# Window values of six sequences: one wide projection per half, kept in DRAM, in place of four narrow ones in each sequence's own turn

## The chip, the cores and the metric

The kernel runs on one core of a Trainium2 chip. The metric is the device time of one execution in microseconds (us); the figure that is compared is the median of several executions. The core has five engines that each run their own list of instructions strictly in order and meet only at semaphores: PE (TensorE, matrix products into PSUM), DVE (VectorE), ACT (ScalarE), POOL (GpSimd) and SP (SyncE, which here only issues DMAs). [...]All data is float32, and each float32 matrix product shows as two PE records in the profile.

## The reference, cut to what matters

One decoder layer on x of shape (8, 256, 256), that is eight sequences of 256 rows and 256 channels: self-attention, cross-attention to a context of the same shape, and a mixture of eight experts, each followed by a sum with its input and a layer norm.

```python
# self-attention: three attentions with the same queries q, weighted by a gate
a1 = _attn(q, k1, v1, causal=True)     # latent keys and values
a2 = _attn(q, ks, vs, causal=False)    # 64 selected rows
a3 = _attn(q, kw, vw, causal=True)     # "window" keys and values
kw = (x @ w_wink)...                   # rope on 64 of 96
vw = (x @ w_winv).reshape(B, T, 16, 32)   # 256 -> 512 channels: 16 heads of 32
out = (g[:, 0] * a1 + g[:, 1] * a2 + g[:, 2] * a3) @ w_proj
x = _layernorm(x + out)
x = _layernorm(x + cross_attention(x, ctx))       # 16 heads of 16
# experts: all eight are computed for every row
h = relu(einsum('btd,edh->bteh', x, W1) + b1)     # 256 -> 1024
y = einsum('bteh,ehd->bted', h, W2) + b2          # 1024 -> 256
x = _layernorm(x + sum over e of router[e] * y[e])
```

The change concerns only `vw = x @ w_winv`. It depends on the layer's input and on one weight, and on nothing that is computed before it.

## The kernel before, in words

**Threads and a planner.** The kernel is written as some thirty generators ("threads"), each a sequence of instructions for one part of the work. When the program is built, a planner (class `Machine`, L119 to L255) walks through them with a small model of each engine's time. At each step it finds for every engine the instruction that could start earliest; among those within 0.1 us of it, it takes the one with the lowest rank number. The result is one fixed list per engine. The hardware then runs these lists in order, so an instruction that is late on the chip holds up all that stands behind it on its engine. A thread may also yield a number, which becomes its rank, or a condition (`seen(...)`) that holds it until another thread has set a mark.

**The ranks.** The self-attention and cross-attention threads of sequence s run at about 1 to 7 plus 4 times s (`AHEAD = 4`, L36), so a lower sequence goes first. `context()` (L1154) has rank 60: it projects keys and values of the context for all eight sequences and keeps them in DRAM. `finish()` has 50. `experts()` (L1387) has 99, so its products fill whatever time PE has left.

**What a sequence needs.** `project()` (L843) handles a sequence in four groups of four heads. For a group it makes q, the window keys and the selected keys, marks `heads`, and then makes the window values of the group: it claims one of two buffers `vw` (128 x 2 x 128), multiplies the two halves of the rows (i) by the group's 128 columns of `wvw` in four products with 128 columns each (k is the half of the contraction), into a PSUM bank `pv`, and copies that to `vw` on DVE or ACT, whichever is free first (`copied`, L294). `products()` (L1063) later multiplies the softmax weights `pa` with `vw` (L1105), with the selected values `vs` and with the latent values `vl`, and then releases `vw`. For the first sequence (s = 0) the weights are turned on PE (`pt`); for all others they are written to DRAM and read back turned, by SP's DMAs `pr<-pr` and `pa<-pr` (`by_dram`, L581; `turned`, L623).

**Buffers that the change touches.** The pool tag "side" has one buffer of 128 x 512; `context()` uses it for `kc` and `vc`, `second()` (L1215) for the cross-attention's queries `qc`, and `fetch()` (L1193) for `vc`. The tag "turn" has two buffers of 128 x 1024, and every rotary step uses one (`turn`, L548): DVE writes it, POOL reads it. The selected values of a sequence or a pair of them leave through a buffer `sv` of its own (L717).

**DMAs.** Every DMA is issued by SP, in one list, and an issue that waits for a buffer holds up the ones behind it. The expert weights come as 256 loads of 512 KB, with two buffers for the halves of W1 and two for those of W2.

Of the kernel before, what the change touches and what calls it, by code (L numbers as in the profile page):

```python
# [17 lines left out]
P = 128  # L18
# [14 lines left out]
NEG = -1e30  # L33
LOWEST = -3.4028234663852886e38
QSCALE = 1.0 / math.sqrt(DH)
AHEAD = 4  # L36
ENGINES = {
    mybir.EngineType.PE,
# [220 lines left out]
def decoder_layer(ctx: ExitStack, tc: tile.TileContext, a: dict, out: bass.AP):  # L259
# [13 lines left out]
    def mm(out, lhsT, rhs, start=True, stop=True, share=1):  # L273
        us = 2 * 0.00084 * max(free_size(rhs), free_size(lhsT)) / share
        return Op(
            "PE",
            us,
            [out],
            [lhsT, rhs],
            lambda: nc.tensor.matmul(out, lhsT, rhs, start=start, stop=stop, skip_group_check=share > 1),  # L280
            lag=0.17,
        )
# [5 lines left out]
    def group(ops, extra=0.0):  # L288
        op = Op("PE", sum(o.us for o in ops) + extra, [], [], lambda: [o.issue() for o in ops], lag=0.17)
        op.writes = list(dict.fromkeys(k for o in ops for k in o.writes))  # L290
        op.reads = list(dict.fromkeys(k for o in ops for k in o.reads))
        return op
# [15 lines left out]
    def mtile(shape, name):  # L308
        return mtile_(shape, "m", name)
# [30 lines left out]
    def kp(x):  # L340
        return x.rearrange("(k p) c -> p k c", p=P)
# [312 lines left out]
    def selection(s, d):  # L654


        xr = xrs[s]
        yield seen("raw", s)
        sc = one([1, T], "sc", "sc")
        yield m.claim(sc)  # L660
        pi = mtile([1, T], "pi")
        yield group([tr(pi[:, bass.ts(i, P)], d["gi"][:, i, 3:4]) for i in range(2)])
        yield copied(sc, pi)
        m.release(pi)
        left = one([1, T], "left", "left")
        for i in range(KEEP // 8):
            m8 = tiny("m8", [1, 8])
            src = left if i else sc
            yield V.max(m8, src)
            yield V.match_replace(left, m8, src, LOWEST)  # L670
        yield V.tensor_tensor(left, left, sc, ALU.not_equal)
        yield V.tensor_tensor_scan(sc, left, left, 0.0, ALU.add, ALU.max)
        yield V.tensor_tensor(sc, sc, left, ALU.mult)
        yield V.tensor_scalar(sc, sc, -1.0, None, ALU.add)
        m.release(left)
        pp = mtile([P, 2], "ppos")
        yield group([tr(pp[:, i : i + 1], sc[:, bass.ts(i, P)]) for i in range(2)])
        m.release(sc)
        pos = tiny("pos", [P, 2])
        yield V.tensor_copy(pos, pp)  # L680
        m.release(pp)
        hot = one([P, 2, KEEP], "left", "hot")
        for i in range(2):
            yield G.tensor_scalar(hot[:, i, :], iota, pos[:, i : i + 1], None, ALU.is_equal)

        n = s - lead(s)
        if n == 0:
            both = d["selT"] = one([P, 2, 2, KEEP], "selT", "selT")
            yield m.claim(both)
            d["users"] = 2  # L690
        else:
            yield lambda: "selT" in pro[s - 1]
            both = pro[s - 1]["selT"]
        pg = mtile([P, 2, KEEP], "psel")
        yield group(
            [
                mm(pg[:, k, :], xr[:, i, bass.ts(k, P)], hot[:, i, :], i == 0, i == 1)
                for k in range(2)
                for i in range(2)
            ]  # L700
        )
        m.release(hot)
        yield V.tensor_copy(both[:, :, n], pg)
        m.release(pg)
        done.add(("selected", s))
        if lead(s + 1) == s:
            return
        rows = (n + 1) * KEEP
        pv = mtile([P, H * VH], "pvs")
        yield group(  # L710
            [
                mm(pv[0:rows], both[:, k, 0 : n + 1].rearrange("p n s -> p (n s)"), wvs[:, k, :], k == 0, k == 1)
                for k in range(2)
            ]
        )
        used(lead(s))
        sv = one([P, H * VH], "sv", "sv")  # L717
        yield copied(sv[0:rows], pv[0:rows])
        m.release(pv)
        pro[lead(s)]["sv"] = dv = kept_in_dram([P, H * VH], f"sv{lead(s)}")  # L720
        yield dma(dv[0:rows], sv[0:rows])
        m.release(sv)
        done.add(("selected values kept", lead(s)))
# [119 lines left out]
    def project():  # L843
        for s in range(B):
            yield 2 + AHEAD * s
            d = pro.setdefault(s, {})
            for g in range(NHG):
                yield seen("latent", s)
                yield seen("parts", g)
                yield seen("latent weights")  # L850
                xT = xTs[s]
                h = {}
                for name, shape in (("q", [P, 3, T]), ("kx", [P, 3, KX]), ("vw", [P, 2, P])):
                    h[name] = two(shape, name, name)
                yield m.claim(h["q"], h["kx"])
                lT = d["lT"]

                pq = mtile([P, 2, T], "pq")
                yield group([mm(pq[:, i], wq[0:QL, 0, g, i], lT[0:QL, :]) for i in range(2)])
                yield from turn([h["q"][:, 0], h["q"][:, 1]], pq, T)  # L860
                m.release(pq)

                pk = mtile([P, 2, T], "pk")
                for i in range(2):
                    yield group([mm(pk[:, i], wkw[:, k, g, i], xT[:, k, :], k == 0, k == 1) for k in range(2)])
                yield from turn([window(h["kx"], 0), window(h["kx"], 1)], pk, T)
                m.release(pk)

                pq = mtile([P, T], "pqn")
                yield mm(pq, wq[0:QL, 0, g, 2], lT[0:QL, :])  # L870
                yield copied(h["q"][:, 2], pq)
                m.release(pq)

                pk = mtile([P, T], "pkm")
                yield group([mm(pk, wkw[:, k, g, 2], xT[:, k, :], k == 0, k == 1) for k in range(2)])
                yield copied(window(h["kx"], 2), pk.rearrange("p (c t) -> p c t", c=2))
                m.release(pk)

                ks = None
                if lead(s) == s:  # L880
                    two_ = lead(s + 1) == s
                    yield seen("selected", s)
                    if two_:
                        yield seen("selected", s + 1)
                        stash = kept[g] = four([P, 3, KEEP], "stash", "stash")
                        yield m.claim(stash)
                    ks = mtile([P, 3, 1 + two_, KEEP], "pks")
                    sel = d["selT"][:, :, 0 : 1 + two_].rearrange("p k n s -> p k (n s)")
                    yield group(
                        [  # L890
                            mm(ks[:, i].rearrange("p n s -> p (n s)"), wks[:, k, g, i], sel[:, k], k == 0, k == 1)
                            for i in range(3)
                            for k in range(2)
                        ]
                    )
                    if g == NHG - 1:
                        used(s)
                    if two_:
                        yield copied(stash, ks[:, :, 1])
                    own = ks[:, :, 0]  # L900
                else:
                    own = kept[g]
                yield from turn([h["kx"][:, i, P:N0] for i in range(2)], own[:, 0:2], KEEP)
                yield copied(h["kx"][:, 2, P:N0], own[:, 2])
                m.release(kept.pop(g) if ks is None else ks)
                heads[s, g] = h
                done.add(("heads", s, g))

                yield m.claim(h["vw"])
                pv = mtile([P, 2, P], "pv")  # L910
                yield group(
                    [
                        mm(pv[:, i], xT[:, k, bass.ts(i, P)], wvw[:, k, bass.ts(g, P)], k == 0, k == 1)
                        for i in range(2)
                        for k in range(2)
                    ]
                )
                yield copied(h["vw"], pv)
                m.release(pv)
                if g == NHG - 1:  # L920
                    m.release(d["lT"])
                done.add(("values", s, g))

    def latent_pairs(name):

# [543 lines left out]
    each(7, gates)  # L1469
    m.thread(5, selected_values())  # L1470
    m.thread(5, context())
    m.thread(5, fetch())
    m.thread(99, experts())
    m.thread(50, finish())
# [96 lines left out]
```

## Time and profile before

| | |
|---|---|
| median of 3 runs | 1673.97 us (1671.38 to 1674.11) |
| profiled execution | 1674.96 us, of which the span from first to last instruction is 1673.2 us |
| PE busy | 1609.5 us, 96% of the span |
| DVE, ACT, POOL busy | 1158.9, 583.8, 599.7 us |
| DMA | 330 MB, 57.6% of 16 engines |
| first expert product `ph` starts | 250.09 us |
| last product `ox` of the eighth sequence's cross-attention | 1512.1 us |

The page divides the span into 40 slices of 41.8 us and gives for each the busy tenths of each engine and the granted PE clock. A PE that is busy is not necessarily at its peak rate: while the clock is halved, the same products take longer and count as busy. "Idle before" and the views of waits give the time in which an engine had nothing running, and what released it. The kernel has three stretches: up to 250 us there are no expert products, since the first sequence has to pass both attentions first; from there to about 1510 us attention of the later sequences is mixed with experts; after that there are hardly any products but the experts'.

### The profile page before, as it was taken

The numbers are of one execution on the slowest core, as the hardware profiler recorded it, in microseconds if no ns is written. First come the engines' busy times: TensorE is split into PE (matmuls) and PEld (weight loads), VectorE is DVE, ScalarE is ACT, GpSimd is POOL, SyncE is SP. The second block draws the span as 40 slices with busy tenths as digits, with TensorE's granted clock in tenths as the row PEclk, the third lists the DMA queues.
The fourth block names the chain that finished last, engine by engine and source line by source line (L and its number), as shares of the span: only waits on it lengthen the run. The fifth ranks groups of instructions, "written<-read, shape, count | busy, mean of one in ns | idle before, by whom it ended". The sixth has DMA issues, their size and how long they took to land.

```text
span 1673.2 us, 31920 instructions
## 1 busy us (share of the span) xinstructions
PE 1609.5 (96%) x12040; PEld 1320.2 (79%) x12040; DVE 1158.9 (69%) x2577; ACT 583.8 (35%) x2114; POOL 599.7 (36%) x795
## 2 busy tenths in 40 slices
PE   6899789999999999999999999999999999999998
PEld 4778568887887778888888688878888778888887
DVE  4968678678789874887678884688767774544333
ACT  2464543244435430434434341244435341220000
POOL 3665753253534430334235332243335332120000
PEclk8999899999999999999999999999999999999999
DMA  6311416378648675655746676566656777585552
GB/s 218 117 50 47 166 69 217 120 245 284 233 141 291 245 248 192 211 205 189 252 172 234 241 249 227 151 238 211 226 196 221 248 257 251 154 307 153 161 156 96
DMA packets 185657, 329.96 MB, mean 197 GB/s; under 512 B 13200, under 2 KB 105504, under 8 KB 178336
## 3 DMA queue, kind: packets, MB, share of 16 engines
q1 hardware_dynamic: 185504, 327.92, 57.6%
q8 instruction: 96, 1.57, 0.4%
q14 instruction: 57, 0.47, 0.1%
HBM read 237.70 MB, written 90.19 MB: 196 GB/s over the span
## 4 chain that ended last, share of the span: by engine, by line
PE 83%; issue 7%; DVE 4%; DMA 3%; POOL 1%; SPq 1%; ACT 0%; POOLq 0%; DVEq 0%; ACTq 0%
PE ph L280 23%; PE py L280 22%; PE s L280 9%; PE o L280 4%; PE pk L280 3%; PE pyo L280 3%; PE ox L280 2%; PE pv L280 2%; PE sx L280 2%; DMA xpt<-prx 1%; PE pkm L280 1%; PE pks L280 1%; PE pq L280 1%; PE pt L286 1%; PE pkr L280 1%
## 5 line engine op out<-in xcount | busy, mean ns | idle before, releaser
L280 PE MATMUL ph<-xT,w 128*128 128x256 f32 x2048 | 475.2, 382 | 3.8 <-DVE pl L98 2.6
L280 PE MATMUL py<-w,h 128*128 128x256 f32 x2048 | 471.5, 381 | 0.0
L280 PEld LDWEIGHTS ph<-xT,w 128*128 128x128 f32 x2048 | 383.8, 190 | 70.2 <-issue 16.7
L280 PEld LDWEIGHTS py<-w,h 128*128 128x128 f32 x2048 | 383.7, 190 | 59.7 <-issue 7.7
L98 ACT ACTIVATE h<-ph,b 128x256 f32<-128x256 f32 x227 | 107.5, 473 | 391.5 <-PE ph L280 340.0
L98 DVE TENSOR_SCALAR h<-ph,b 128x256 f32<-128x256 f32 x285 | 136.9, 482 | 112.5 <-PE ph L280 109.6
L98 DVE SCALAR_TENSOR_TENSOR xr<-py,rw,xr 128x256 f32<-128x256 f32 x128 | 61.2, 478 | 174.7 <-PE py L280 174.6
L98 POOL TENSOR_TENSOR prx<-prx,sumsx 128x512 f32<-128x512 f32 x128 | 130.6, 1051 | 118.8 <-DVE sumsx L98 73.2
L98 ACT ACTIVATE prx<-sx,nmx 128x256 f32<-128x256 f32 x256 | 117.0, 486 | 43.3 <-DVE nmx L98 41.9
L98 POOL TENSOR_TENSOR pr<-pr,wpr 128x256 f32<-128x256 f32 (+2 forms) x128 | 129.4, 1042 | 0.0
L98 POOL TENSOR_TENSOR rstd<-var,nhalf 128x2 f32<-128x2 f32 x24 | 17.4, 725 | 310.0 <-DVE var L98 309.9
L98 ACT ACTIVATE pl<-pl,nmpl 128x128 f32<-128x128 f32 (+1 forms) x256 | 113.1, 446 | 30.6 <-DVE nmpl L98 29.9
L98 POOL TENSOR_TENSOR kx<-turn 128x64 f32<-128x64 f32 (+1 forms) x128 | 65.3, 527 | 162.6 <-DVE turn L98 156.9
L98 ACT ACTIVATE pr<-pr,nmpr 128x128 f32<-128x128 f32 (+1 forms) x256 | 113.2, 447 | 0.0
L98 DVE TENSOR_TENSOR pr<-s,causal 128x256 f32<-128x256 f32 x128 | 74.6, 583 | 41.0 <-PE s L280 34.6
L280 PE MATMUL s<-kx,q 32*128 32x320 f32 (+1 forms) x1536 | 96.1, 390 | 0.3 <-POOL kx L98 0.3
L98 POOL TENSOR_TENSOR pl<-pl,wpl 128x512 f32<-128x512 f32 x64 | 93.1, 1475 | 2.7
L98 POOL TENSOR_TENSOR q<-turn 128x256 f32<-128x256 f32 x64 | 45.8, 735 | 134.1 <-DVE turn L98 130.8
L280 PEld LDWEIGHTS s<-kx,q 32*128 32x128 f32 x1536 | 71.2, 189 | 17.8 <-issue 7.1
L98 DVE TENSOR_REDUCE nmx<-sx 128x2 f32<-128x512 f32 x128 | 79.1, 678 | 8.5 <-PE sx L280 8.5
L98 DVE TENSOR_TENSOR pl<-s,causal 128x256 f32<-128x256 f32 x128 | 74.3, 581 | 12.6 <-PE s L280 8.6
L98 DVE TENSOR_REDUCE nmpr<-pr 128x4 f32<-128x256 f32 (+2 forms) x128 | 80.5, 673 | 0.0
(217 smaller groups left out, 2385.1 us busy)
## 6 DMA issues: line engine op xcount, KB each, us to landing
w<-in_W SPq DMA_DIRECT2D x256, 512.0 KB, 4.2
pr<-pr SPq DMA_DIRECT2D x28, 1024.0 KB, 4.1
pa<-pr SPq DMA_DIRECT2D x28, 1024.0 KB, 6.9
prx<-prx SPq DMA_DIRECT2D x28, 1024.0 KB, 5.2
xpt<-prx SPq DMA_DIRECT2D x28, 1024.0 KB, 6.5
pl<-pl SPq DMA_DIRECT2D x28, 768.0 KB, 4.9
pb<-pl SPq DMA_DIRECT2D x28, 768.0 KB, 7.2
xT<-in_xT SPq DMA_DIRECT2D x8, 256.0 KB
```

The lines of the kernel that those rows point to most:

```text
L98: return Op(self.name, us, outs, ins, lambda: getattr(self.engine, kind)(*args, **kw))
L280: lambda: nc.tensor.matmul(out, lhsT, rhs, start=start, stop=stop, skip_group_check=share > 1),
L286: return Op("PE", 0.11, [out], [in_], lambda: nc.tensor.transpose(out, in_, ident[:n, :n]), lag=0.17)
```

## The change

The window values of sequences 0 and 1 are made as before. For sequences 2 to 7 (`EARLY = 2`) a new thread `values()` with rank 61 makes them ahead of time. As soon as the weights of the context are there (mark "ctx weights"), it loads the sequence's transposed input once more into a new buffer `vT`, and for each half of the rows makes one PSUM bank of 128 x 512 with two products (all 16 heads at once), copies it on ACT into the one "side" buffer, and writes it to DRAM (256 KB). `project()` then issues, in place of the four products and the copy, one DMA that reads the group's 128 columns of both halves into `vw`. To make room for `vT`, `sv` moves from a buffer of its own to one of the two "turn" buffers.

```diff
+EARLY = 2
 ...
-        sv = one([P, H * VH], "sv", "sv")
+        sv = two([P, H * VH], "turn", "sv")
 ...
                 yield m.claim(h["vw"])
-                pv = mtile([P, 2, P], "pv")
-                yield group([mm(pv[:, i], xT[:, k, bass.ts(i, P)], wvw[:, k, bass.ts(g, P)], k == 0, k == 1)
-                             for i in range(2) for k in range(2)])
-                yield copied(h["vw"], pv)
-                m.release(pv)
+                if s < EARLY:
+                    (the same as before)
+                else:
+                    yield seen("values kept", s)
+                    yield dma(h["vw"], vws[s][:, :, bass.ts(g, P)])
 ...
+    vws = {}
+
+    def values():
+        for s in range(EARLY, B):
+            yield 61
+            yield seen("ctx weights")
+            xT = one([P, 2, T], "vT", "vT")
+            yield dma(xT, kp(a["xT"][:, bass.ts(s, T)]))
+            d = vws[s] = kept_in_dram([P, 2, H * VH], f"vw{s}")
+            for i in range(2):
+                pv = mtile([P, H * VH], "pv")
+                yield group([mm(pv, xT[:, k, bass.ts(i, P)], wvw[:, k], k == 0, k == 1) for k in range(2)])
+                vw = one([P, H * VH], "side", "vw")
+                yield A.copy(vw, pv)
+                m.release(pv)
+                yield dma(d[:, i], vw)
+                m.release(vw)
+            m.release(xT)
+            done.add(("values kept", s))
 ...
     m.thread(5, context())
+    m.thread(5, values())
     m.thread(5, fetch())
```

More of the change, by code (lines that the diff above doesn't have):

```diff
@@ L909, in project @@
                 yield m.claim(h["vw"])
-                pv = mtile([P, 2, P], "pv")
[L911 to L917, printed above, removed]
-                yield copied(h["vw"], pv)
-                m.release(pv)
+                if s < EARLY:
+                    pv = mtile([P, 2, P], "pv")
+                    yield group(
+                        [
+                            mm(pv[:, i], xT[:, k, bass.ts(i, P)], wvw[:, k, bass.ts(g, P)], k == 0, k == 1)
+                            for i in range(2)
+                            for k in range(2)
+                        ]
+                    )
+                    yield copied(h["vw"], pv)
+                    m.release(pv)
+                else:
+                    yield seen("values kept", s)
+                    yield dma(h["vw"], vws[s][:, :, bass.ts(g, P)])
                 if g == NHG - 1:
@@ L922, in project @@
                 done.add(("values", s, g))
+    vws = {}
[11 more added lines that the diff above has]
+                yield A.copy(vw, pv)
+                m.release(pv)
+                yield dma(d[:, i], vw)
+                m.release(vw)
+            m.release(xT)
+            done.add(("values kept", s))
     def latent_pairs(name):
```

## The prediction

> **What bounds the kernel now.** I began with the page, parts 1 and 2.
>
> ```profile
> PE 1609.5 (96%) x12040; PEld 1320.2 (79%) x12040; DVE 1158.9 (69%) x2577; ACT 583.8 (35%) x2114; POOL 599.7 (36%) x795
> ...
> PE   6899789999999999999999999999999999999998
> ...
> PEclk8999899999999999999999999999999999999999
> ```
>
> PE is busy for 96% of the span. Of its 63.7 us of idle time (1673.2 - 1609.5) most lies in the first seven slices, and only there is the clock below 9. So I cut that stretch up and set a later one beside it (columns: stretch, then busy us of PE, weight loads, DVE, ACT and POOL, granted clock, DMA share, GB/s).
>
> ```profile
> 50.00:100.00 50.00, 44.29 (x390) 36.21 (x389) 43.26 (x116) 29.95 (x109) 37.90 (x53) 0.93 0.29 89
> 100.00:150.00 50.00, 47.31 (x518) 38.53 (x520) 38.43 (x105) 26.29 (x88) 29.57 (x36) 0.97 0.14 50
> 150.00:200.00 50.00, 42.39 (x347) 32.76 (x340) 36.10 (x74) 27.24 (x102) 32.67 (x45) 0.90 0.41 145
> 200.00:250.00 50.00, 42.20 (x432) 32.33 (x431) 36.87 (x80) 25.70 (x98) 26.82 (x34) 0.92 0.16 60
> ...
> 600.00:800.00 200.00, 197.81 (x1380) 164.22 (x1380) 142.78 (x328) 64.42 (x237) 63.41 (x83) 1.00 0.62 209
> ```
>
> From 50 to 250 us PE is idle for 5.7 + 2.7 + 7.6 + 7.8 = 23.8 us, and the halved clock takes (0.07 + 0.03 + 0.10 + 0.08) x 50 = 14 us more. Those 38 us are what work without a deadline could fill. From 600 to 800 us only 2.2 of 200 us are idle: there every us of PE work taken away is a us won. The waits of PE up to 260 us and after it say who causes the idle time (us in total, times, longest).
>
> ```profile
> PE ptx L286 <- DVE xr L98: 5.2, 1, 5.2
> ...
> PE plt L286 <- DVE lat L98: 5.1, 2, 2.7
> PE o L280 <- DMA pa<-pr: 4.4, 1, 4.4
> PE pt L286 <- POOL pr L98: 3.7, 3, 1.7
> ...
> PE sx L280 <- ACT prx L98: 1.9, 1, 1.9
> ```
> ```profile
> PE ox L280 <- DMA xpt<-prx: 4.5, 4, 1.9
> PE ph L280 <- DVE pl L98: 2.6, 2, 1.6
> ```
>
> Early there are waits of the first sequence's chain. Later there is nearly nothing, and no product `ph` or `py` ever waits for a weight's DMA.
>
> **Part 1: PE work removed.** Six sequences x 4 groups = 24 groups `pv` of 4 products (8 records). Their cost is the distance to the next group's start (a record's duration overlaps the next).
>
> ```profile
> 424.40 1.16 PE L280 MATMUL pv<-wvw,xT 128*128 128x128 f32 x8
> 425.49 0.71 PE L280 MATMUL pvl<-wkv,lk 32*128 32x128 f32 x8
> ```
> ```profile
> 301.48 1.88 PE L280 MATMUL pvs<-wvs,selT 128*128 128x512 f32 x4
> 303.20 1.05 PE L280 MATMUL pv<-wvw,xT 128*128 128x128 f32 x8
> 304.18 2.06 PE L280 MATMUL s<-kx,q 32*128 32x192 f32 x36
> ```
>
> That is 1.09 and 0.98 us; with 1.0, 24.0 us. All 24 lay behind 250 us, where experts fill PE, so all of it counts.
>
> **Part 2: PE work added.** 12 groups of two products 128 x 512. The group `pvs` has exactly this shape: 303.20 - 301.48 = 1.72 us, so 20.6 us. In the planned order all 12 stand before the first `ph`. If nothing is recovered, the trade is 20.6 - 24.0 = -3.4 us.
>
> **Part 3: what the added work covers.** I read this from the planned order of PE, wait by wait.
> - `ptx` (5.2 us, at 243 us): before, only the cross-attention's projection stood ahead of it; now `pk`, `pqn`, `pkm` and a context projection too, 0.86 + 0.43 + 0.87 + 1.73 (distances of starts) = 3.9 us.
> - `plt` of the second sequence (2.7 of the 5.1 us, at 117 us): a values group stands ahead of it, 1.7 us.
> - `sx` (1.9 + 0.7 us, at 188 us): a values group, the second sequence's `psel` and context work now stand between the `sx` groups, 2.6 us.
> - `pt` (3.7 us, at 67 us): POOL's constant fill of `xq` (2.80 us) stood before the first `pr` weighing and now stands behind it, 2.8 us. Against that, 4.5 us of other PE work (`pqn`, `pkm`, `xpv`, `pks`) that stood ahead of `pt` is replaced by one values group; it isn't lost, but the cover is thinner, so I count only 1.5 us.
> - `ox` (1.4 + 0.8 us): score groups stand between now, 1.5 us.
> - `o` (4.4 us, at 194 us): its values group stands behind it, so nothing.
>
> The sum is 11.2 us of idle time. For the clock there is a row and a rule. The row: after the 4.4 us wait the clock was 0.52 from 190 to 200 us, and `pv` at 198.32 took 1.87 us to the next start instead of 1.0; over 50 to 250 us it cost 14 us for 24 us of waits. The rule: the Trainium skill, "TensorE: Matmul & The Clock Gate", section "What's actually happening", says that the clock halves after an idle window of some 3.4 us and comes back after as much work. By it only the two waits above 3.4 us should cost, some 1.7 us each, 3.4 us in all; the row, 0.58 us of clock per us waited, would return 6.5 us for 11.2. The waits that I shorten are mostly below 3.4 us, so I take 3 us, nearer the rule: -11 - 3 = -14 us.
>
> **Part 4: what the added work costs elsewhere.**
> - ACT: 12 copies 128 x 512 at 0.585 us (row `vc<-xpv`), 7.0 us before 250 us, where ACT is busy for 109 of 200 us. ACT and DVE lose 24 copies of 0.372 or 0.424 us later. Cover: ACT's free half. But each copy waits for the one "side" buffer, and the softmax exponentials stand behind it on ACT. The nearest row is the context's `kc`, written by 16 ACT instructions into the same buffer: before `kc` work ACT and POOL sat idle for 9.4 us with no releaser shown and for 2.1 us until a DMA out of "side" (`cq<-qc`) had landed, 11.5 / 16 = 0.7 us for each. Bounds for 12 copies: 0 to 9 us. I take 3 us, since PE had other groups to run in most of these places.
> - SP: 18 more issues before 250 us and 24 later, 0.45 us each, 19 us of an engine with room. The `vT` load waits for PE to read the last one and the writes wait for ACT; behind them stand context loads and the second sequence's `pr` and `pa`. 0 to 5 us; I take 1.
> - The 24 reads of `vw` (128 KB) replace the products. Each waits for the products two groups earlier to release its buffer. In the planned order of SP each stands 11 to 44 entries ahead of the `pa` read that the same products need, and `pa` itself waits for a later release. Reads of 128 KB (`vs<-sv`) land in 3.0 us. So `o` isn't held up. A rule against it: the Trainium skill, "Perfetto Trace Analysis", "DMA Optimizations", warns that small DMAs (under 2 KB) have significant overhead; these rows are 512 B, those of `vs` 2 KB. By the row it costs 3 us of latency, by the rule perhaps twice that (an estimate); with at least one `pa` landing (6.9 us) of lead both come out at nothing.
>
> ```profile
> vs<-sv SPq DMA_DIRECT2D x16, 128.0 KB, 3.0
> ck<-kc SPq DMA_DIRECT2D x8, 256.0 KB, 2.0
> ```
>
> - DMA volume: 12 x 256 + 6 x 256 + 24 x 128 KB = 7.9 MB on 330 MB, most of it where the DMA share is 0.14 to 0.41. Nothing.
> - `sv` in "turn": five times a rotary buffer is held for a copy (0.6 us) and a write (2.4 us). Twice before 250 us the other buffer alone serves DVE and POOL; up to 2 us, I take 0. Later experts cover it.
> - The whole plan shifts, since it is one greedy list. Idle time after 260 us is 15 us before; I allow 4 us either way and take 0.
>
> **The sum:** -3.4 - 14 + 3 + 1 = -13.4 us against the profiled 1674.96 us (span 1673.2 and 1.8 around it), 1661.6. The median shown is 1.0 us lower; I forecast 1661.
>
> **The rivals.**
> - *Nothing is recovered (1666 to 1675).* The added groups take their full 20.6 us in a stretch where PE is already busy for 88%, and the waits only move behind them, since they come from latency the planner doesn't know. For it: the longest wait, `pa<-pr`, keeps its place. Against it: for the other four, work now stands ahead. Time: -3.4 + up to 4 of stalls, 1672.
> - *All of it is recovered (1645 to 1653).* The 20.6 us run inside the 38 us of idle and slow time. Then -24.0 counts alone, 1650. Against it: a group of 1.72 us in a gap of 1 us pushes the rest.
> - *Slower (1677 to 1700).* ACT is held at the "side" buffer. Each of the 12 copies waits until the write before it has landed (2.0 us by the `ck` row), and with it the exponentials behind it, so the first sequence's chain is late and new waits of PE open where there are no experts to fill them. The gain without stalls is 17.4 us, so it decides from 17.4 / 12 = 1.5 us of PE wait per copy; at 2.5 us it is +12.6 us, 1687. For it: ACT and POOL already idle before `kc`, and `context()` needs the same buffer 16 times. Against it: ACT has half its time free, and PE has the second sequence's work.
>
> **How the numbers follow.** Chances: forecast (1653 to 1666) 0.43, nothing recovered 0.25, all recovered 0.12, slower 0.20. A measurement of this kernel tells about 0.2%, 3.3 us, from no change; faster means below 1670.6. "Nothing recovered" is split evenly by it: 0.12 faster, 0.13 the same. So faster 0.67, same 0.13, slower 0.20. For 8 in 10 the range leaves out the lower half of "all recovered" and the upper part of "slower": 1649 to 1682. The likeliest case's own range is 1653 to 1666.
>
> **What would show it.** Right: 8 instead of 32 `pv` groups of 128 columns and 12 of 512, all before the first `ph`; PE idle from 50 to the first `ph` at 14 us or less; the wait of `ptx` near 1 us; no product `o` waiting for a read of `vw`; the first `ph` some 10 to 15 us later than 250 us, with more of the second sequence done. Wrong: ACT idle for over 1.5 us before the new copies on a DMA, PE idle before 300 us above 40 us, or `ph` waiting for weights because a `vw` read blocks SP.

## The result, and the profile after

The changed kernel took **1686.43 us** (median of 6 executions, 1680.44 to 1691.28), the kernel before beside it 1673.46 us (6 executions, 1671.38 to 1674.95). The ratio is **1.0077**, 95% interval 1.0056 to 1.0099: the change makes the kernel 0.8% slower, where 1661 us had been forecast. The profiled execution took 1691.28 us with a span of 1689.4 us, against 1674.96 and 1673.2 before.

The page's first two parts of the changed kernel, the lines that answer to those shown of before:

```profile
PE 1618.7 (96%) x11896; PEld 1312.4 (78%) x11896; DVE 1178.0 (70%) x2582; ACT 577.6 (34%) x2097; POOL 600.3 (36%) x795
...
PE   5989978999999899999999999999999999999998
...
PEclk8999989999899899999999999999999999999999
```

PE has 144 records fewer, as the removal of 24 groups of 8 and the addition of 12 groups of 4 make it, and yet it is busy for 9 us longer. The row of the clock says why: it now falls below 9 in two slices far behind the first `ph`, the eleventh and the fourteenth. The mean granted clock went from 0.986 to 0.977. A slower clock makes the same products longer, and they count as busy.

The stretches (columns as in the prediction: stretch, busy us of PE, weight loads, DVE, ACT and POOL, granted clock, DMA share, GB/s):

```profile
50.00:100.00 50.00, 42.34 (x348) 31.91 (x348) 40.03 (x108) 25.77 (x94) 31.52 (x41) 0.86 0.30 87
100.00:150.00 50.00, 50.00 (x505) 38.27 (x503) 38.61 (x113) 31.08 (x105) 28.29 (x40) 1.00 0.16 52
150.00:200.00 50.00, 48.38 (x436) 36.34 (x436) 38.27 (x75) 23.73 (x79) 23.48 (x33) 1.00 0.45 139
200.00:250.00 50.00, 38.77 (x319) 27.97 (x318) 26.62 (x57) 25.86 (x99) 28.12 (x33) 0.86 0.41 139
```

From 100 to 200 us PE hardly idles any more: there the added groups did what they were forecast to do. But from 50 to 100 and from 200 to 250 us it idles for 7.7 and 11.2 us, more than before (5.7 and 7.8), at a lower clock. From 45 us to the first `ph` (250.1 us before, 276.2 us now) 23.8 us of idle time and 13.7 us of clock (half of the time at half clock, from the trace's clock record) were lost before, 26.0 and 14.0 us after. Where both fall together and are counted once, that is 33.8 us before and 37.0 us after (the 38 us of the prediction counted that part twice). The first `ph` is 26 us later, which is the added work (20.6 us), one more group of the second sequence, and these 3 us. Nothing was covered on balance.

The waits of PE in the changed kernel, over the whole span (us in total, times, longest):

```profile
PE xpk L281 <- DVE pl L99: 6.5, 1, 6.5
PE ppos L287 <- DVE sc L99: 4.5, 1, 4.5
PE s L281 <- ACT prx L99: 4.0, 1, 4.0
PE o L281 <- ACT pr L99: 3.3, 1, 3.3
...
PE ptx L287 <- DVE xr L99: 2.3, 2, 1.7
```

The old waits did shrink: `ptx` from 5.2 to 1.7 us at its longest, and the waits from 40 to 280 us for `lat` and for `pa<-pr` are gone. Four others stand in their place. Two are early (`ppos` at about 93 us, `xpk` at 220 us), two are far behind the first `ph`. PE's instructions behind these last two (start, us, what, idle before and its releaser), and then the stretches around them (same columns as above):

```profile
423.22 1.00 PE L281 MATMUL s<-lx,q 32*128 32x128 f32 x9 [4.01 <-ACT prx L99]
...
563.47 1.51 PE L281 MATMUL o<-pa,vw 128*32 128x256 f32 x16 [3.30 <-ACT pr L99]
```

```profile
420.00:430.00 10.00, 6.78 (x48) 5.37 (x49) 6.34 (x12) 3.75 (x16) 1.30 (x2) 0.61 0.97 336
430.00:440.00 10.00, 10.00 (x87) 7.36 (x86) 6.34 (x14) 3.76 (x13) 5.41 (x6) 0.88 0.38 125
...
560.00:570.00 10.00, 6.70 (x64) 4.58 (x61) 9.86 (x22) 4.48 (x19) 3.12 (x4) 0.61 0.27 93
570.00:580.00 10.00, 10.00 (x64) 7.63 (x63) 6.80 (x13) 1.61 (x4) 4.22 (x4) 0.88 0.76 259
```

Each of the two waits, 4.0 and 3.3 us, goes with another (0.39 + 0.12) x 10 = 5.1 us of clock, some 0.5 us of it still within the wait. From 400 to 600 us, where before lost 3.1 us of idle time at full clock, the changed kernel loses 10.8 us of idle time and 10 us of clock. Two more stretches of half clock of 3.4 us each, from 961.5 and from 1337.0 us, are too short to show in the page's digits; before has one such, from 941.4 us. From the first `ph` to 1400 us idle time and clock, counted once, lost 18.6 us before and 36.3 us after: 3.8 us more of idle time (17.1 and 20.9) and some 14 us more of clock. So the ledger of the profiled pair: the trade -3.4, the early stretch +3, the late one +18, some +17 where +16.3 was measured.

### The profile page after: what moved, and what is told of

It reads as the page before. It is cut to its first block, busy times and chain, and to the rows that moved or that the text cites. A ratio compares the mean times of both kernels' runs of the same rounds, so it can differ in the third digit from the quotient of the medians.

```text
span 1689.4 us, 31698 instructions
## 1 busy us (share of the span) xinstructions
PE 1618.7 (96%) x11896; PEld 1312.4 (78%) x11896; DVE 1178.0 (70%) x2582; ACT 577.6 (34%) x2097; POOL 600.3 (36%) x795
## 4 chain that ended last, share of the span: by engine, by line
PE 77%; DVE 8%; issue 7%; DMA 4%; POOL 2%; SPq 1%; ACT 0%; POOLq 0%; DVEq 0%; ACTq 0%
PE ph L281 21%; PE py L281 21%; PE s L281 8%; PE o L281 4%; PE pk L281 3%; PE pyo L281 2%; PE pq L281 2%; PE sx L281 2%; PE ox L281 2%; DMA prx<-prx 1%; PE pks L281 1%; PE pv L281 1%; PE pkm L281 1%; PE pt L287 1%; DVE pr L99 1%
## 5 line engine op out<-in xcount | busy, mean ns | idle before, releaser
L281 PE MATMUL ph<-xT,w 128*128 128x256 f32 x2048 | 480.2, 385 | 0.4 <-ACT prx L99 0.4
L99 DVE TENSOR_SCALAR h<-ph,b 128x256 f32<-128x256 f32 x314 | 151.0, 482 | 115.8 <-PE ph L281 113.0
L99 ACT ACTIVATE h<-ph,b 128x256 f32<-128x256 f32 x198 | 93.5, 473 | 331.7 <-PE ph L281 302.3
L281 PE MATMUL s<-kx,q 32*128 32x192 f32 (+1 forms) x1536 | 93.9, 383 | 0.3 <-POOL kx L99 0.2
L99 DVE TENSOR_TENSOR pl<-s,causal 128x256 f32<-128x256 f32 x128 | 74.5, 582 | 11.2 <-PE s L281 9.5
```

The costliest lines, as they stand in the source:

```text
L99: return Op(self.name, us, outs, ins, lambda: getattr(self.engine, kind)(*args, **kw))
```

## The experiments

Three theories, named so in the expectations. **A**: the trade of work is as forecast, and what is lost is lost to new waits, because the plan made another order on all engines. **B**: the loss comes from the early stretch itself, from the shared buffer "side", from SP, or from the disturbed chain of the first sequence. **C**: the reads from DRAM cost time.

### One half of the change at a time

Removal alone: the 24 groups are replaced by reads, there is no values thread, and `sv` keeps its buffer. The rows are read from the weight, so the values of six sequences are not the right ones.

```diff
+                    yield dma(h["vw"], kp(a["w_winv"])[:, :, bass.ts(g, P)])
-    m.thread(5, values())
```

> The products and copies of the window values of sequences 2 to 7 are left out: the group's columns are read from the weight w_winv instead (same pieces of 512 B, same 24 DMAs), and no values are computed ahead, so those sequences' window attention uses wrong values. This is the removal alone. Theory A (the trade holds, and what was lost is new waits that any reshuffled plan can have): 24 us less, 1649, give or take 8 for the plan. Theory B (the loss is in the early stretch, from the shared buffer and SP's queue): 24 us less, 1649, closely. Theory C (the reads themselves cost: SP is blocked, or the groups had been useful filling): about 10 us less or nothing, 1663 to 1673.

Measured: 1670.66 us (1665.91 to 1674.41, 11 executions), ratio 0.998 (0.9967 to 0.9992). Only 3 us of the 24 came, where A and B expected them all; the time is one that C named.

Addition alone: the changed kernel with its values thread, but all sequences still compute their values themselves and nothing reads the rows in DRAM.

```diff
-                if s < EARLY:
+                if s < B:
```

> The values of sequences 2 to 7 are computed ahead and written to DRAM as in the change, but nobody reads them: every group still makes its own. This is the addition alone, sv in a rotary buffer included. Theory A: the 20.6 us of products without cover, 1694, give or take 8. Theory B: 20.6 us and some 16 us of waits in front of the first expert product, 1710. Theory C: about 20 us, 1694, closely. If the early gaps had covered the products after all: below 1685.

Measured: 1706.59 us (1703.89 to 1713.91, 4 executions), ratio 1.0197 (1.0166 to 1.0228): 33 us for 20.6 us of work. That is nearest to B's 1710. Each half comes out 12 to 21 us worse than its instructions. As both make a new plan, these two runs can't say whether the halves or the plan are to blame.

### The order alone

The plan charges 2.5 us for the way of a transfer. With 2.4 or 2.6 the kernel before does the same work in another order. The plan also decides anew what DVE and what ACT takes: with 2.4, 318 of the 512 `h` are made on DVE, before 285. "Order" below includes that.

```diff
-            end = self.transfers + 2.5
+            end = self.transfers + 2.4
```

> The kernel before with one number of the planner changed (the latency it assumes for a DMA, 2.4 instead of 2.5 us), so that only the order of instructions shifts; the work is the same. Theory A: the time moves by up to 8 us either way, and the single long waits of PE are other ones. Theories B and C: within 3 us of before, 1670 to 1677.

> The kernel before, whose planner takes 2.6 us for a transfer's way instead of 2.5: same work, another order. Theory A: 1680 to 1695, as with 2.4 (1689.87). If the order of before is nothing special: within 5 us of 1673.7.

Measured: with 2.4, 1689.87 us (1683.7 to 1693.32), ratio 1.0081 (1.0053 to 1.011); with 2.6, 1688.61 us (two executions), ratio 1.0091 (1.0066 to 1.0116). The order alone costs 15 to 16 us in both; for 2.4, theory A had allowed 8. With 2.4 the first `ph` stands at 252.8 us, so at most 3 us of it are in the early stretch. Most of it is clock: the mean granted clock is 0.978, in before 0.986, and 0.008 x 1689 us are some 13 us. Two of the waits of PE in that run, over the whole span:

```profile
PE ox L280 <- DVE pl L98: 5.3, 1, 5.3
...
PE sx L280 <- DVE pl L98: 4.7, 1, 4.7
```

Neither is there in before. The first stands at 960 us: one long wait in the midst of the experts' time, as the changed kernel has them. The order of before is better than both of its neighbours, and an edit that makes a new plan can lose it.

The changed kernel with the same two constants:

> The changed kernel with the same number of the planner changed (2.4 instead of 2.5 us). Theory A: another time than the changed kernel's 1686 by some us, anywhere from 1665 to 1690. Theories B and C: within 3 us of 1686.

> The changed kernel with 2.6 us instead of 2.5. Its distance to the kernel before with 2.6 us is the change with another draw of the order on both sides. By the pairs so far (+13 at 2.5, +9.5 at 2.4) between 0 and +15 us. If the change is worth its sum of -13 us and only the order of before hides it, it is below its partner in some pair.

Measured: with 2.4, 1699.41 us (1696.52 to 1701.16), ratio 1.015 (1.0133 to 1.0167), 9.5 us above its partner. With 2.6 one execution took 1716.66 us, 28 us above its partner's median; a second, of 1756.44 us, ran at a mean granted clock of 0.928 instead of 0.973 and is not compared. Both times lie above what had been expected (up to 1690, and up to 15 us over the partner). The change loses in each of three draws of the order. Three draws, one of them a single execution, are few beside a spread of 15 us, but they speak against the luck of before being the whole of it.

### The removal in the order of before

The plan still sees the group and its copy at their old costs. When it comes to issue them, the group issues nothing, and the copy issues the read. Every engine's list is then that of before, less the 24 groups and copies, plus 24 reads on SP where the copies stood; in the trace PE, DVE, ACT and POOL run their instructions in the order of before, but for those left out. The values are those of the removal alone, not the right ones.

```diff
+                    same = group([...])
+                    same.issue = lambda: None
+                    yield same
+                    both = copied(h["vw"], pv)
+                    for op in both:
+                        op.issue = lambda v=h["vw"], g=g: nc.sync.dma_start(out=v, in_=...)
+                    yield both
```

> The removal alone, like the run with reads only (1670.66 us, 3 us below before), but every engine's order stays that of before: the 24 groups and their copies are left out where they stood, and the 24 reads stand on SP where the copies stood. The values read are not the right ones. Theory A (the order of before is a rare good one, and reordering ate the removal's 24 us): about 1650 us, 1647 to 1654, the whole 24 us. Theory C (the reads themselves cost, as waits of the products or on SP): no better than the run with reads only, 1665 to 1675, with waits of `o` on the DMA of vw in the chain of waits.

Measured: **1652.56 us** (1652.37 to 1654.39), ratio 0.9879 (0.9861 to 0.9898), that is 21.0 us below before, where the same removal with a new plan brought 3. The page of this run:

```profile
PE 1587.3 (96%) x11848; PEld 1299.2 (79%) x11848; DVE 1153.5 (70%) x2568; ACT 578.6 (35%) x2099; POOL 599.7 (36%) x795
```

PE is busy for 22.2 us less than before. Theory C falls, since the 24 reads are all in this kernel. The 18 us between the two removals are the new order's. (`sv` keeps its own buffer in both, so the move of `sv` is not needed for such a loss.)

### The values in the experts' time

```diff
-            yield seen("ctx weights")
+            yield seen("normed", 0)
```

> As the changed kernel, but the values wait for the first sequence's normed rows instead of the context weights, so the 12 groups run in the experts' time and not in the early stretch. Nothing is covered by early waits, so the trade is -3.4 us. Theory A: the order shifts here too, for some +15 us: 1680 to 1690. Theory B (the loss comes from the early stretch: the shared buffer, the first sequence's chain): 1668 to 1673, as nothing early is touched, and the first ph near 250 us.

Measured: 1684.92 us (1684.44 to 1689.19), ratio 1.0077 (1.0054 to 1.01), the ratio of the changed kernel itself. The first `ph` starts at 252.0 us, so the early stretch is as before, and the loss is there all the same. One of its waits of PE, over the whole span, stands at 940 us:

```profile
PE sx L281 <- DVE pl L99: 8.0, 1, 8.0
```

From 600 to 1400 us this run idles for 15.4 us (before 11.6), and its clock is 0.98 from 600 to 1000 us. Theory B does not explain this kernel.

### The shared buffer

The changed kernel in its own order, but the rows on their way to DRAM lie in buffers that the experts use only later; the planner still books "side" for them. One copy becomes two of half the width, and one write two.

```diff
-                vw = one([P, H * VH], "side", "vw")
+                vw, more = like_side("vw0"), sb.tile([P, T], F32, tag="h", name="vw1", bufs=8)
```

> The changed kernel in its own order on every engine, but the rows on their way to DRAM lie in buffers that the experts use only later (two copies of 128 x 256 and two writes per group), not in side; the planner still books side for them, so that the order stays. If the shared buffer is a cause (ACT idle for 8.3 us before `vc` at 208 us until `ck` had landed, then PE idle for 6.5 us before `xpk`), both waits shrink and the time falls by 5 to 10 us, to 1676 to 1682. If the order alone is it, within 3 us of the changed kernel's 1686.4, since the same instructions stand in the same queues.

Measured: 1689.73 us (1684.88 to 1693.72), ratio 1.0098 (1.0079 to 1.0116), no better than the changed kernel. One of the waits of ACT from 45 to 276 us in this run, then one of PE's in the same stretch:

```profile
ACT vc L99 <- DMA ck<-kc: 9.7, 1, 9.7
```
```profile
PE xpk L281 <- DMA cT<-in_ctxT: 9.9, 2, 9.3
```

The pair of waits (208 to 220 us in the changed kernel, 203 to 216 us here) is still there, though no row of the new thread is in that buffer. It is `context()`'s own chain: `vc` waits until `kc` has left "side", and the `cT` load stands behind the issue of `ck` on SP. What SP waits for there, and what POOL does in that time (start, us, what):

```profile
SPq L272 <- POOL kc L99: 10.9, 1, 10.9
```
```profile
199.18 4.03 POOL L99 TENSOR_TENSOR prx<-prx,sumsx 128x512 f32<-128x512 f32 x4
...
204.78 4.02 POOL L99 TENSOR_TENSOR pr<-pr,wpr 128x512 f32<-128x512 f32 x4
208.77 0.59 POOL L99 TENSOR_TENSOR kx<-turn 128x64 f32<-128x64 f32 x2
209.33 1.26 POOL L99 TENSOR_TENSOR kc<-kc,keep 128x512 f32<-128x512 f32 x1
```

The masking of `kc` on POOL stands in the plan behind two weighings of 4.0 us each. So this price is the order's, not the sharing's.

### The whole change in the order of before

Now the added part is set in without the plan's knowledge: its instructions take no time and no buffers in the plan, and each is issued as soon as the plan has come to the time at which it could run. The rows lie in the experts' buffers, as above; the removed part is handled as in the removal in the order of before. These values are the right ones.

```diff
+                pv = unseen(ps, "m", 8, [P, H * VH], "pv8")
+                yield free_of_cost(group([...]), 0.0)
+                vw = [unseen(sb, "h", 8, [P, T], "vwh") for k in range(2)]
+                for k in range(2):
+                    yield free_of_cost(A.copy(vw[k], pv[:, bass.ts(k, T)]), 0.0)
```

> The whole change, right values, but with every engine's order that of before: the 12 groups of values, their copies, loads and writes are set in where the plan of before has come to by the time they can run, and are nothing to the planner; the reads stand where the copies stood, as in the run with reads in the order of before (1652.56 us). The rows lie in buffers that the experts use only later (tag h, two copies of 128 x 256 and two writes per group instead of one), so nothing waits for the buffer side, and sv keeps its own. Theory A (the change is as forecast and lost by the new order): 1652.6 + 20.6 added less what early waits cover (11 to 14 us) = 1659 to 1663. Nothing recovered: 1652.6 + 20.6 = 1673. Theory B (the addition disturbs the first sequence's chain wherever it is put): above 1675.

> The addition alone in the order of before: as the run with the whole change in that order, but the 24 groups pv and their copies are computed as before and nothing reads the rows kept in DRAM. The addition alone with its own new order cost 33 us (1706.59). Theory A: 1673.5 + 20.6 - 11 to 14 = 1680 to 1683. Nothing recovered: 1694. Theory B: above 1697.

Measured: the whole change 1676.91 us (1675.65 to 1681.04), ratio 1.0037 (1.0022 to 1.0051); the addition alone 1693.98 us (1692.37 to 1698.88), ratio 1.0143 (1.0125 to 1.016), that is 22.1 us for 20.6 us of work. The halves, -21.0 and +22.1, add up to +1.1; together they measured +5.0, and I have no cause for the other 4 us. The addition alone is where "nothing recovered" had it (1694); the whole change is just inside the range of theory B (above 1675). In this order nothing is covered either. Four waits of PE from 40 to 300 us in the run with the whole change say why:

```profile
PE ptx L297 <- DVE xr L99: 5.2, 1, 5.2
PE pv L291 <- DMA vT<-in_xT: 4.2, 2, 2.9
PE o L291 <- DMA pa<-pr: 4.0, 1, 4.0
PE pbo L291 <- POOL wide L99: 3.4, 1, 3.4
```

The groups ran as soon as they could, all by 157 us; the long waits come after that (here `o` at 215 and `ptx` at 265 us) and are nearly as long as in before. The early waits that the groups did shorten (`pt`, `plt`, `sx`) were paid for with new ones: `pv` waits twice for its own load `vT`, and `pbo` for POOL. To that extent B is right for this run. Work without a deadline that is done at the first chance covers nothing that comes later.

### The groups set at the waits

The same kernel, but each group is issued just in front of the instruction of PE that waits in before. `AT` counts PE's steps in the plan: 43 is the first `pt`, 89 `plt`, 161 the `sx` at 187 us, 162 the `o` at 194 us, 173 `ox`, 203 `ptx`. The values are the right ones.

```diff
+    AT = [43, 43, 89, 89, 161, 162, 162, 162, 173, 203, 203, 203]
+            yield lambda: m.npe >= at - 1
```

> The whole change in the order of before again (right values), but each of the 12 groups is set by hand just in front of the instruction of PE that waits in before: two before the first `pt` (waits 3.7 us), two before `plt` (2.7), one before the `sx` at 187 us (1.9), three before the `o` at 194 us (4.4), one before `ox` (1.4), three before `ptx` (5.2). In the run with the whole change in the order of before (1676.91 us) the groups had all run by 157 us, and `ptx` and `o` still waited 5.2 and 4.0 us. Theory A (those waits are latency that PE work can cover, as the prediction's Part 3 says, and the early groups were only in the wrong place): 1652.6 + 20.6 - 17 of idle time, and some 3 of clock = 1651 to 1660. If what PE waits for is itself behind PE work, so that the waits move on: 1670 to 1678, with the waits still in the trace.

> The same with another placing by hand: two before the first `pt`, one each before `plt`, before the `sx` at 179 us and the `sx` at 187 us, two before the `o` at 194 us, one before `ox`, one before the score group `s` at 222 us, three before `ptx`. Theory A: within 4 us of the other placing, 1651 to 1662, since two of the groups stand where PE waits less. Waits that move on: 1670 to 1678.

Measured: **1662.47 us** (1657.46 to 1670.79, 8 executions; before beside it 1674.83), ratio **0.9941** (0.9916 to 0.9965), and with the other placing, `AT = [43, 43, 89, 157, 161, 162, 162, 173, 189, 203, 203, 203]`, 1663.43 us (1660.2 to 1666.51), ratio 0.9935 (0.991 to 0.9961). Both beat both kernels; both lie 1 to 3 us above the range that theory A gave (up to 1660 and 1662), and far below 1670. The first placing's stretch, then PE's instructions at two of the places (start, us, what):

```profile
50.00:250.00 200.00, 188.46 (x1685) 140.46 (x1687) 154.65 (x372) 111.30 (x398) 123.51 (x164) 0.98 0.30 102
```
```profile
192.59 7.12 PE L293 MATMUL pv<-wvw,vh 128*128 128x512 f32 x12
199.63 0.86 PE L293 MATMUL o<-pa,vw 128*32 128x256 f32 x16
...
243.12 5.31 PE L293 MATMUL pv<-wvw,vh 128*128 128x512 f32 x12
248.35 0.87 PE L299 MATMUL ptx<-ident,xr 128*128 128x128 f32 x4
```

`o` and `ptx` start at once behind three groups each; neither carries a wait any more. From 50 to 250 us PE idles for 11.5 us instead of 23.8, at a clock of 0.98 instead of 0.93. The first `ph` starts at 252.9 us, 2.8 us later than before with 20.6 us more work done: 17.8 us were covered. (Against the removal alone in this order, whose first `ph` is at 248.8 us, it is 16.5 us.)

## Why the prediction was wrong

**The failed step is the last of Part 4**: "The whole plan shifts, since it is one greedy list. Idle time after 260 us is 15 us before; I allow 4 us either way and take 0." The same work in two other orders measured 15 and 16 us above before, and the late stretch of the changed kernel lost 18 us more than that of before. The bound was set on the idle time that before had there. A new order isn't bounded by that: it brings waits that before didn't have, and the long ones cost the clock as well.

**Part 3, as a sum, failed with it.** It read from the planned order what now stands ahead of each old wait, and there it was right: `ptx` fell to 1.7 us (about 1 was forecast), and the waits for `lat` and `pa<-pr` went. But it took the new plan's own new waits at nothing, and `xpk`, `ppos` and their like gave all of it back (37.0 us lost up to the first `ph`, before 33.8). That such waits can be covered at all is shown by the groups set at them: 17.8 us, with 11.2 of idle time and 3 of clock forecast. Between that kernel and the same change in the same order, placed at the first chance, lie 14.4 us by medians (16 by ratios): that is the place of the groups alone. From there to the changed kernel it is another 7 us by ratios or 10 by medians, where order and place both differ.

**The clock term, 3 us, was mis-sized.** With the groups at the waits, 12.3 us less idle time from 50 to 250 us went with (0.98 - 0.93) x 200 = 10 us less clock loss (the two digits of the clock leave some 2 us open). The row of before, 0.58 us per us waited, makes that 7; the rule of the Trainium skill, "TensorE: Matmul & The Clock Gate", "What's actually happening", makes it 3.4 (an estimate). I had weighed row against rule and gone with the rule, since most of the waits were below 3.4 us. The trace of before already showed that those cost as well: half clock for 3.4 us behind the `plt` wait of 2.7 us (118.8 to 122.2 us), and for 6.8 us at the two `pt` waits of 1.7 and 1.5 us (67.6 to 74.4 us). The half clock that I laid to the 4.4 us wait began at 190.4 us, 0.4 us after PE had stopped, so the `sx` waits before it had their part. The two late waits of the changed kernel speak against the rule again, with some 4.6 us each behind the wait (worked out in the last section) where one window at half clock is 1.7; they cost more than by the row, too. But the same 3.3 us wait cost nothing in another run, so neither prices a single wait.

**Part 1 and Part 2 held.** The removal was 24.0 us by the sum and 21.0 measured, 0.87 us per group instead of 1.0. The added group was 1.72 us by the sum; three of them take 248.35 - 243.12 = 5.23 us in the last extract, and 12 uncovered ones cost 22.1 us.

**Of the rest of Part 4**, that no `o` waits for a read of `vw` was right, and so was the DMA volume. Of the row and the rule for these reads the row held: in the run with the whole change in the order of before they land in 2.8 us, as the 3.0 of `vs` had it, and not in twice that.

```profile
vw<-vw SPq DMA_DIRECT2D x24, 128.0 KB, 2.8
```

ACT did idle before the new copies, but mostly for PE. Two of its waits from 45 to 276 us in the changed kernel:

```profile
ACT vw L99 <- PE pv L281: 13.9, 5, 9.3
...
ACT vw L99 <- DMA ck<-kc: 1.9, 2, 1.5
```

With the buffer taken out of the way the time was no lower, so the 3 us for ACT were not the matter. SP's 1 us and `sv` in "turn" were not measured by themselves.

**The rivals.** The time of the slower rival, 1687, came true within 1 us, by another mechanism: it said that ACT is held at "side", and the run without that sharing is no faster. That the time fits is luck. "Nothing is recovered" describes the early stretch best, but its 1672 lacks the late loss.

**What stays open.** With the groups at the waits, removal and the later first `ph` make 1673.5 - 21.0 + 2.8 = 1655 us, and 1662 to 1663 was measured. Profile against profile the gap nearly closes: the removal alone in the order of before took 1652.37 us, the run with the groups at the waits 1659.46. Of these 7.1 us, 4.1 stand before the first `ph` (248.8 and 252.9 us), and 2.6 are idle time from there to 1400 us (17.5 and 20.1 us). The median of 1662.47 lies another 3 us above the profiled execution, for no cause that I know. I did not find what makes the order of before so good, only that two small turns of a constant lose it. Nor did I hold the changed kernel's own order and move its groups alone.

## What to carry to other kernels

Where a planner writes the order of in-order engines, the order is a variable of its own: turn a constant that should not matter and see how far the time moves (here by 1%), and judge an edit with the order held, or over several orders. Work without a deadline covered waits here where it stood directly in front of the instruction that waits; set in at the first chance, it covered nothing. Its place in the plan's time is not its place on the chip. A gain of some 1% that needs a new plan should be priced with the spread of plans, not with zero.

## What was not expected of the hardware

In the changed kernel a single wait of 3.3 or 4.0 us slowed PE for much longer than itself. The granted clock around the wait that ended at 423.22 us in the changed kernel (same columns, 1 us each):

```profile
421.00:422.00 1.00, 0.00 (x0) 0.00 (x0) 0.74 (x2) 0.00 (x0) 0.30 (x1) 1.00 0.95 401
422.00:423.00 1.00, 0.00 (x0) 0.00 (x0) 1.00 (x1) 0.85 (x4) 0.00 (x0) 0.61 1.00 406
...
431.00:432.00 1.00, 1.00 (x4) 0.82 (x3) 1.00 (x4) 0.47 (x1) 0.81 (x2) 0.50 0.06 25
432.00:433.00 1.00, 1.00 (x10) 0.47 (x13) 0.90 (x1) 0.24 (x1) 1.00 (x2) 0.77 0.06 25
```

PE stopped at 419.2 us; the clock fell at 422.2, 3 us later, and came back at 432.5, only 9.3 us after PE had begun to work again. At half clock that costs 4.6 us. The wait of 3.3 us at 560 us went the same way, half clock from 562.2 to 572.4 us.

The length of a wait does not fix its price, though. In the run whose rows lie in buffers of their own the same `o` waits for the same 3.30 us, and the clock stays up:

```profile
559.03 0.86 PE L281 MATMUL o<-pa,vw 128*32 128x256 f32 x16 [3.30 <-ACT pr L99]
```
```profile
560.00:570.00 10.00, 9.79 (x95) 7.30 (x88) 10.00 (x23) 3.84 (x16) 3.01 (x3) 1.00 0.86 274
```

In before, on the other hand, two short waits close together were enough for half clock from 941.4 to 944.8 us, while single waits of 1.8 and 1.9 us (at 536 and 1100 us) left the clock up:

```profile
939.11 1.10 PE L280 MATMUL ph<-xT,w 128*128 128x256 f32 x4 [1.06 <-DVE pl L98]
941.82 1.94 PE L280 MATMUL ox<-xpt,vx 128*32 128x256 f32 x16 [1.60 <-DMA xpt<-prx]
```
```profile
942.00:943.00 1.00, 1.00 (x12) 0.41 (x11) 0.95 (x1) 0.26 (x2) 0.00 (x0) 0.50 0.00 0
```

The stretches of half clock behind such waits lasted 3.4 us (941.4 to 944.8 us in before), 6.8 us (67.6 to 74.4) or 10.2 us (422.2 to 432.5 in the changed kernel). So a wait of 3.3 us cost between nothing and some 5 us of clock, and the cost is read from the clock column, not from the wait. An order with few and short waits is worth more than its idle time says: the clock takes 23 us in before (0.014 of 1673) and 39 us in the changed kernel (0.023 of 1689).
